# Layer 1 of a four-layer decoder: head-strided attention as steps behind each batch's self-attention

## The chip, the cores and the metric

The kernel runs on one core of a Trainium2 chip. The metric is the device time of one execution in microseconds (us); the reported time is the median of several runs. Engines are named as in the profile: PE multiplies matrices (PEld is its weight load), DVE, ACT and POOL are the vector, scalar and general-purpose engines, SP issues loads and stores. "L568" is line 568 of the kernel before.

## The reference, cut to what matters

The whole is a decoder of four layers. Each layer applies three residual steps to `x` (4 batches of 256 rows by 128 columns): a self-attention, a cross-attention to a context of 4 x 512 rows, and a feed-forward part. The change touches layer 1, whose first two steps are these (16 heads of 8 columns):

```python
def _L1_attn_ref(x, Wqkv, Wout):
    q, k, v = ...                                   # 16 heads, no biases
    scores = jnp.einsum('bhtd,bhsd->bhts', q, k) * SCALE
    scores = jnp.clip(scores, -10.0, 10.0)
    mask = jnp.triu(jnp.full((t, t), NEG), k=1)
    attn = jax.nn.softmax(scores + mask, axis=-1)
    out = jnp.einsum('bhts,bhsd->bhtd', attn, v)
    return out.reshape(b, t, d) @ Wout.T

def _L1_xattn_ref(hidden_states, key_value_states, Wq, bq, Wk, bk, Wv, bv, Wo, bo, stride):
    Q, K, V = ...                                   # projections with biases, 16 heads
    idx = jnp.arange(H)[:, None] + stride * jnp.arange(m)[None, :]
    Kg, Vg = ...                                    # head h sees only keys h, h + 16, h + 32, ...
    attn = jax.nn.softmax(jnp.einsum('bhqd,bhkd->bhqk', Q, Kg) * scaling, axis=-1)
    out = jnp.einsum('bhqk,bhkd->bhqd', attn, Vg)
    return out.reshape(B, Tq, E) @ Wo.T + bo

x = x + _L1_attn_ref(_layernorm(x), L1_attn_Wqkv, L1_attn_Wout)
x = x + _L1_xattn_ref(_layernorm(x), ctx_1024, ..., 16)
x = x + _L1_ffn_ref(_layernorm(x), ...)             # 8 experts, the best 2 per row
```

In the head-strided attention every head sees 32 of the 512 keys, so 16 heads by 32 keys give 512 scores per query row.

## The kernel before

All data stay on the chip as float32: `x` is one tile of 128 partitions by 8 row tiles, two per batch, and the transposed context `cT` has been made in layer 0. The layers run one after the other. Layer 1 is called by `layer_1` (L1753, the self-attention), then `strided_attention` (L1216), then `ffn1` (L1148, the experts). Each stage opens its own pools of on-chip tiles and of PSUM buffers (the banks that PE writes), and closes them at its end.

The self-attention is written by `woven` (L432). A unit is one batch. Its `prelude` (L648) normalises the batch (`normalised_T`, L311), transposes it and projects queries (L449) and keys (L460). Queries are kept four times, each copy multiplied on POOL by a mask that leaves one head of every four (L458). `columns_of` (L547) makes scores with the keys on the partitions: four PE tiles at a time (L568), DVE clips them against -10 and 10 or the causal mask (L578), ACT takes the exponential (L583). `weighted` (L598) multiplies by the values (L604), ACT copies the sums (L610), and `divided_by_sums`, `transposed_result` and `added` (L612 to L646) divide, transpose, project with the output weights (L639) and add to `x` (L643). One batch in layer 1 has two pairs of key-tile groups: in each pair, first a group whose four tiles have 512 score columns, then one with 256, because the causal mask removes the rest.

The order of the steps is a list of (time, function) pairs. `back` (L720) gives the scores of a unit their beats within 0 to 1, and the later steps times after them, each later by a `step`, one beat of the unit; items at or after 1 are carried into the next unit (L750 to L759). All score tiles and other short PSUM tiles of this stage use one set of seven buffers named `s1`. A scheduler then orders the instructions of every engine by their readiness as it estimates it, except those marked with `keep_in_program_order`. [...]

`strided_attention` builds keys and values for all batches first. Keys are spread into blocks, so that one product gives the scores of four heads (`kbd`, L1223 to L1239), and so are values (`vbd`, L1241 to L1265). The query weights are padded: each head has 32 columns, of which 8 are filled, so the query projection is four products per batch (`project`, L336) and DVE adds the bias and scales four times (`padded_queries`, L328). Then, for each of a batch's two row tiles: four score products (L1273), the maximum (L1279) and its subtraction (L1281) on DVE, the exponential on ACT (L1285), four transposes (L379), four products with the values (L1289), division, transposition, output product and addition (`divided`, L360, and `finish`, L352).

The weights of layers 1 to 3 are loaded by `loads` (L1789), eight transfers issued one after the other on ACT within the prelude of the third batch of layer 1: `w1x`, `e1h`, `e1d`, `w2a`, `w2x`, `w3a`, `w3x`, `w3f`. `ternary_weights` (L1647) is called at the end of `linear_attention` (layer 2). It begins with two sums of absolute values of `w3f` on DVE (L1653), which the scheduler may place anywhere after that load was issued.

## Time and profile before

| | us |
|---|---|
| median of 3 runs | 1777.98 (1774.26 to 1781.84) |
| the profiled execution | 1781.78 |
| its span in the profile | 1780.0 |

| engine | busy us | share of the span |
|---|---|---|
| PE | 1459.3 | 82% |
| PEld | 783.2 | 44% |
| DVE | 870.1 | 49% |
| ACT | 694.4 | 39% |
| POOL | 337.2 | 19% |

The clock granted to PE was 0.86 of full speed over the span. The stages around the change, as the timeline shows them: the last write of layer 0's experts is issued at about 384 us, the first score columns of layer 1 begin at 415.5 us, the self-attention's results are added to `x` at 462.6, 476.4, 492.6 and 498.4 us, the last strided result at 582.6 us, and the first product of the experts begins at 608.1 us.

A line of the timeline gives start, duration, engine, line, operation, output and inputs, shapes and count, and in square brackets how long the engine had been idle before it and what released it. A line of the groups gives line, engine, operation, names, shapes and count, then the busy time in us and the mean duration in ns, then the idle time just before it with its releasers. PE counts a float32 product as two instructions and a transpose as one. The chain of waits lists start, duration and what the last-ending chain of work did there.

### The profile page before, as it was taken

Reading aid. Unit: us, or ns where it says so; the run is one execution under the profiler, and the core shown is the slowest. Engines: PE = TensorE matmul, PEld = TensorE weight load, DVE = VectorE, ACT = ScalarE, POOL = GpSimd, SP = SyncE. Lnnn points to the kernel's source line nnn. Section 1 sums busy time; section 2 is a strip of 40 time slices with the busy share of each in tenths; the row PEclk is TensorE's granted clock in tenths of the full one; section 3 lists DMA queues with packets and bytes.
Section 4 is the critical chain, followed back from the end, with each engine's and each line's share of the span. In section 5 each row is a group of like instructions: output and inputs, shape, how many; then the busy total and the mean of one; then the engine's idle time right before and its main releaser. Section 6 shows DMA issues by size and latency. Waiting matters only on the chain.

```text
span 1780.0 us, 27163 instructions
## 1 busy us (share of the span) xinstructions
PE 1459.3 (82%) x10180; PEld 783.2 (44%) x10180; DVE 870.1 (49%) x2888; ACT 694.4 (39%) x1380; POOL 337.2 (19%) x494
## 2 busy tenths in 40 slices
PE   5999987964877694557899999999959569999973
PEld 3443333642356363443444554555536334433322
DVE  5676634332644444547534434444233356765426
ACT  1546562322521131002657565666612114444440
POOL 4231102534130223422000000000023242311000
PEclk9999997986766697558999999999979759999985
DMA  7000002325000111000000000000031200000000
GB/s 283 2 1 1 2 1 111 71 47 221 19 1 0 29 38 27 12 1 7 1 0 1 1 1 1 1 1 1 1 117 43 56 13 2 1 1 2 1 2 11
DMA packets 27183, 50.40 MB, mean 28 GB/s; under 512 B 4275, under 2 KB 20955, under 8 KB 25259
## 3 DMA queue, kind: packets, MB, share of 16 engines
q1 hardware_dynamic: 21902, 30.15, 4.8%
q0 software_dynamic: 4000, 8.20, 2.4%
q10 hardware_dynamic: 1152, 10.33, 1.4%
q8 instruction: 82, 1.34, 0.3%
q14 instruction: 47, 0.39, 0.1%
HBM read 40.96 MB, written 7.70 MB: 27 GB/s over the span
## 4 chain that ended last, share of the span: by engine, by line
PE 70%; DVE 12%; ACT 5%; POOL 5%; DMA 3%; issue 3%; ACTq 0%; POOLq 0%; DVEq 0%
PE s L568 6%; PE g L1014 6%; PE o L604 6%; PE s L503 5%; PE o L1575 5%; PE s L1555 5%; PE f L1504 4%; PE y L1035 3%; PE s L555 3%; PE f L1462 2%; PE f L1490 2%; PE s L562 2%; PE t L1024 2%; POOL back L1077 2%; PE s L1548 1%
## 5 line engine op out<-in xcount | busy, mean ns | idle before, releaser
L568 PE MATMUL s<-qm,kc 32*128 32x512 f32 (+1 forms) x896 | 219.2, 619 | 12.8 <-DVE cl L578 12.8
L503 PE MATMUL s<-kc,qm 32*128 32x256 f32 (+1 forms) x1024 | 219.0, 568 | 11.5 <-POOL qm L458 6.5
L585 ACT ACTIVATE pr<-s 128x512 f32<-128x512 f32 x256 | 138.0, 596 | 196.6 <-PE s L568 192.9
L294 POOL TENSOR_SCALAR ve<-mv 128x2 f32<-128x2 f32 (+1 forms) x64 | 14.9, 233 | 832.4 <-DVE mv L292 768.0
L510 DVE TENSOR_REDUCE mx<-s 128x1 f32<-128x512 f32 (+1 forms) x192 | 122.6, 684 | 73.1 <-PE s L568 60.2
L1515 ACT ACTIVATE ss<-ss,ntop 128x768 f32<-128x768 f32 x128 | 118.6, 927 | 100.5 <-DVE ntop L1513 100.2
L604 PE MATMUL o<-pr,v 128*32 128x256 f32 (+1 forms) x1792 | 145.0, 394 | 10.7 <-ACT os L610 5.4
L1509 DVE CUSTOM_DVE_ANT_0 ss<-f,n 128x512 f32<-128x512 f32 x128 | 83.7, 688 | 80.2 <-PE f L1504 80.2
L503 PEld LDWEIGHTS s<-kc,qm 32*128 32x128 f32 x1024 | 89.7, 210 | 66.3 <-issue 18.5
L1575 PE MATMUL o<-pr,v 128*64 128x256 f32 x768 | 112.5, 400 | 0.0
L514 DVE CUSTOM_DVE_ANT_0 junk<-s,nmif 128x512 bf16<-128x512 f32 x128 | 82.9, 688 | 54.8 <-PE s L503 54.5
L1555 PE MATMUL s<-qT,kT 64*128 64x256 f32 x768 | 106.4, 391 | 0.0
L994 POOL DMA_INDIRECT xb<-sent,token x85 | 80.7, 949 | 135.8 <-PE t L1001 59.1
L458 POOL TENSOR_SCALAR qm<-q,consts 128x256 f32<-128x256 f32 x80 | 72.5, 923 | 172.7 <-ACT q L455 119.5
L587 ACT ACTIVATE pr<-s,n 128x512 f32<-128x512 f32 x128 | 80.0, 689 | 55.3 <-PE s L568 36.3
L604 PEld LDWEIGHTS o<-pr,v 128*32 128x32 f32 x1792 | 40.4, 110 | 118.3 <-issue 83.1
L1562 ACT ACTIVATE pr<-s,n 128x512 f32<-128x512 f32 x128 | 80.5, 678 | 27.7 <-PE s L1555 27.6
L562 PE MATMUL s<-mT,selg 12*128 12x256 bf16 x768 | 82.2, 279 | 2.2 <-ACT mT L283 0.7
L568 PEld LDWEIGHTS s<-qm,kc 32*128 32x128 f32 x896 | 70.9, 201 | 22.9 <-DVE cl L578 14.8
L1504 PE MATMUL f<-kT,qT 64*128 64x512 f32 x256 | 78.5, 627 | 2.4 <-ACT kT L283 1.2
L1026 DVE COPY hT<-t 128x512 f32<-128x512 f32 (+1 forms) x85 | 48.0, 565 | 64.4 <-PE t L1024 64.4
L1575 PEld LDWEIGHTS o<-pr,v 128*64 128x64 f32 x768 | 49.1, 138 | 62.7 <-issue 32.7
(381 smaller groups left out, 2642.5 us busy)
## 6 DMA issues: line engine op xcount, KB each, us to landing
e0h<-in_e0h SPq DMA_DIRECT2D x8, 1024.0 KB, 17.3
done<-ys SPq DMA_DIRECT2D x19, 256.0 KB, 2.8
e0d<-in_e0d SPq DMA_DIRECT2D x1, 4096.0 KB
e1h<-in_e1h ACTq DMA_DIRECT2D x1, 4096.0 KB
w2x<-in_w2x ACTq DMA_DIRECT2D x1, 2050.0 KB
e1d<-in_e1d ACTq DMA_DIRECT2D x1, 2048.0 KB, 17.7
e2h<-in_e2h SPq DMA_DIRECT2D x1, 2048.0 KB, 8.4
e2d<-in_e2d SPq DMA_DIRECT2D x1, 2048.0 KB, 13.8
```

The costliest lines, as they stand in the source:

```text
L503: T.matmul(sc[:, i, :], lhsT=u.qm[r, g + i, qt * P : (qt + 1) * P], rhs=u.kc[r, :], start=u.row_mask is None, stop=True,)
L510: V.tensor_reduce(u.mx[:, qt, j, g : g + per], sc, AX.X, ALU.max)
L562: T.matmul(sc[:, i, :], lhsT=selg[r, gp + i, :], rhs=u.mT[r, :], start=u.cols_mask is None and i == 0, stop=False,)
L568: T.matmul(sc, lhsT=u.kc[r, kt * P : (kt + 1) * P], rhs=u.qm[r, gp : gp + 2, first:], start=u.clip, stop=True,)
L585: A.activation(dst, sc, AF.Exp)
L604: T.matmul(u.po[gp][32 * j : 32 * j + 32, i, first:], lhsT=u.v[:, kt, 4 * j + gp + i, :], rhs=u.pr[gp, kt, j][:, i, first:], start=kt + i ...
L1014: T.matmul(p, lhsT=xbT[b], rhs=wh[:, bass.ds(at_h + 512 * i, 512)], start=biases is None, stop=True,)
L1504: T.matmul(sc[h], lhsT=qT[u, c][hrow[h], qt * P : (qt + 1) * P], rhs=kT[u, c][hrow[h], :SK], start=True, stop=True,)
L1509: V.tensor_tensor_reduce(ss[qt][h][:, :SK], sc[h], neg1[:, b * SK : (b + 1) * SK], 1.0, -3e38, ALU.add, ALU.max, accum_out=mx[:, qt, h, 1:2],)
L1515: A.activation(ss[qt][h], ss[qt][h], AF.Exp, bias=ntop[:, qt, h, c : c + 1], accum_out=total[:, qt, h, c : c + 1],)
L1555: T.matmul(sc[h][:, i, :], lhsT=kT[u, c][hrow[h], kt * P : (kt + 1) * P], rhs=qT[u, c][hrow[h], :], start=False, stop=i == 1,)
L1575: T.matmul(po[u, g][hrow[h], i, :], lhsT=v[u][:, kt, n * hd : (n + 1) * hd], rhs=pr[u, g, kt, h][:, i, :], start=kt + i == 0, stop=kt + i ...
```

## The change

- The head-strided attention is no stage of its own any more. `strided_keys` gives steps that prepare keys and values; they are put beside the scores of the first two batches. `strided_steps` gives nine steps per batch, which are put behind the batch's self-attention (`u.after`), spread over 0.9 of a unit. They use the `s1` buffers and the tiles of the self-attention's stage.
- Queries are no longer padded: one product per batch, ACT adds the bias and scales (`q`), POOL multiplies by the four masks (`qs`). Heads are assigned to blocks in another order, so value and output weights are permuted on the host.
- Both row tiles of a batch share one division, one transposition step and one addition.
- In `back`, the distance between the later steps is half a beat where a unit has four beats or fewer. Carried items may be carried again.
- The two sums of `ternary_weights` are kept in program order.
- `w1x` (now 257 KB instead of 644 KB) is loaded by SP at the end of layer 0's experts, `w2x` by ACT within the second batch of the linear attention, into the memory that the experts of layer 1 leave. The six other loads are put beside the scores of the third batch.

```diff
+            u.beside, u.after = [], []
...
+            out += spread(units[n].beside, 0.0, 1.0)
...
             step = 1.0 / most
+
+            lag = step if len(out) > 4 else 0.5 * step
...
-                late += [(at, call(weighted, u, gp, kt, 0)), (at + step, call(weighted, u, gp, kt, 1))]
+                late += [(at, call(weighted, u, gp, kt, 0)), (at + lag, call(weighted, u, gp, kt, 1))]
...
+            late += [(at + lag, call(transposed_result, u)), (at + 2 * lag, call(added, u))]
+            late += spread(u.after, at + 2.1 * lag, at + 2.1 * lag + 0.9)
...
-            own, late, step = back(n)
-            run(own + front(n) + carried + [i for i in late if i[0] < 1.0])
+            own, late = back(n)
+            items = own + front(n) + carried + late
+            run([i for i in items if i[0] < 1.0])
...
-            carried = [((at - 1.0) * following, f) for at, f in late if at >= 1.0]
+            carried = [((at - 1.0) * following, f) for at, f in items if at >= 1.0]
...
+        def source():
+            u["xnT"] = normalised_T(b, pool, tag="s1", on=G)
+            add_bias(2 * b, 5)
+            add_bias(2 * b + 1, 5)
+
+        def queries():
+            q = pool.tile([P, S], F32, tag="q", name="q")
+            A.activation(
+                q, product(w[:, 0:128], u["xnT"], "s1"), AF.Identity, bias=q_bias, scale=SCALE8
+            )
+            u["q"] = pool.tile([P, 4, S], F32, tag="qs", name="qs", bufs=1)
+            for g in range(4):
+                G.tensor_scalar(u["q"][:, g, :], q, gmask[:, g : g + 1], None, ALU.mult)
+
+        def scores(qt):
+            sc = ps("s1")
+            for g in range(4):
+                T.matmul(
+                    sc[:, g * P : (g + 1) * P], lhsT=u["q"][:, g, qt * P : (qt + 1) * P],
+                    rhs=kbd[:, g, b].rearrange("p j k -> p (j k)"), start=True, stop=True,
+                )
+            sv = sc.rearrange("p (h k) -> p h k", h=H)
+            nm = small.tile([P, H], F32, tag="nmh", name="nmh")
+            V.tensor_reduce(nm, sv, AX.X, ALU.max, negate=True)
+            p = u["p", qt] = pool.tile([P, 512], F32, tag="p", name="p")
+            V.tensor_tensor(
+                p.rearrange("p (h k) -> p h k", h=H), sv,
+                nm.unsqueeze(2).to_broadcast([P, H, nj]), ALU.add,
+            )
+            A.activation(p, p, AF.Exp)
...
+        return [
+            source, queries, call(scores, 0), call(scores, 1), call(turned, 0), call(turned, 1),
+            weighted, turned_back, added,
+        ]
...
         for m in range(2):
-            V.tensor_reduce(
+            tc.keep_in_program_order(V.tensor_reduce(
                 sums[:, m : m + 1], w3f[:, m * 512 : (m + 1) * 512], AX.X, ALU.add,
                 apply_absolute_value=True,
-            )
+            ))
...
-            units[2].prelude.append(loads)
+            kbd, vbd, prepare = strided_keys(pool, w)
+            units[0].beside = prepare[:3]
+            units[1].beside = prepare[3:]
+            units[2].beside = [loads]
+            q_bias = scaled(pool, w[:, 512:513])
+            for u in units:
+                u.after = strided_steps(pool, w, q_bias, kbd, vbd, u.b)
             woven(pool, units, S)
...
+        w1x = load("w1x", pool=late, on=nc.sync)
+
+        def loads():
+            for k in ("e1h", "e1d", "w2a", "w3a", "w3x", "w3f"):
+                held[k] = load(k, pool=experts if k[0] == "e" else late, on=A)
+
+        layer_1(w1x, loads)
+        w2a, w3a, w3x, w3f = (held[k] for k in ("w2a", "w3a", "w3x", "w3f"))
+        ffn1(held["e1h"], held["e1d"])
+    with tc.tile_pool(name="w2x", bufs=1) as experts:
+        other(linear_attention)
+        latent_attention(held["w2x"])
```

The steps `turned`, `weighted`, `turned_back` and `added` do for both row tiles what L379, L1289, `divided` and `finish` did for one, and `strided_keys` does what L1223 to L1265 did, in steps of two block groups of keys and of one batch of values.

## The prediction

> **What bounds the kernel now.** I read the page first (busy shares, slices, chain), then the windows of the stretch that the change touches, then the timeline inside it. Everything else keeps its instructions in the same order: layer 0, its experts, layer 3 and the last feed-forward are untouched in the compiled order. On the page PE is busy 82% of the span, but the clock row drops in the slices that hold this stretch, so it is read by itself:

> ```profile
> 415.50:448.90 33.40, 19.07 (x115) 7.94 (x114) 10.62 (x26) 8.60 (x20) 6.15 (x8) 0.70 0.75 310
> 448.90:498.40 49.50, 41.77 (x348) 20.12 (x348) 32.00 (x93) 27.47 (x59) 6.43 (x11) 0.82 0.01 1
> 498.40:582.90 84.50, 64.76 (x288) 51.93 (x288) 37.76 (x97) 13.50 (x34) 14.72 (x33) 0.63 0.00 0
> ```

> The columns are stretch, length, busy time of PE, PE weight loads, DVE, ACT, POOL, then the granted clock, DMA share, GB/s. First row: self-attention of layer 1 from its first score columns on, with PE busy 19.1 of 33.4 us. Second: the rest of it, PE busy 84% at clock 0.82; PE and its hand-offs set the pace. Third: the head-strided attention, PE busy 77% at only 0.63.

> The first row is poor because of one wait. The chain of waits and the timeline:

> ```profile
> 424.49 23.21 DMA w3f<-in_w3f
> ```

> ```profile
> 447.72 1.28 DVE L1653 TENSOR_REDUCE sums<-w3f 128x1 f32<-128x512 f32 x2 [17.84 <-DMA w3f<-in_w3f]
> 449.65 2.41 PE L568 MATMUL s<-qm,kc 32*128 32x256 f32 x6 [12.83 <-DVE cl L578]
> ```

> A reduction for the ternary weights of the *last* layer stands early in DVE's queue and waits for the last of eight weight loads. DVE is idle for 17.84 us, then PE for 12.83 us because DVE frees no score buffers. The groups of the strided stage:

> ```profile
> L340 PE MATMUL sc<-xnT,w1x 128*128 128x256 f32 x32 | 14.5, 610 | 0.0
> L1289 PE MATMUL ms<-vbd,pT 128*128 128x36 f32 x64 | 13.7, 378 | 4.1 <-DVE pT L281 2.3 <-ACT pT L283 1.8
> L1273 PE MATMUL sc<-kbd,qT 128*128 128x128 f32 x64 | 13.3, 370 | 2.0 <-DVE qT L333 2.0
> L379 PE MATMUL pt<-consts,p 128*128 128x128 f32 x32 | 7.3, 373 | 5.3 <-ACT p L1285 5.3
> L1248 PE MATMUL ms<-w1x,kg 128*128 128x32 f32 x32 | 7.1, 353 | 1.4 <-POOL kg L1247 1.3
> L333 DVE TENSOR_SCALAR qT<-sc,w1x 128x256 f32<-128x256 f32 x16 | 6.7, 477 | 14.0 <-PE sc L340 14.0
> ```

> [...]

> **The change part by part.**

> *Ternary sums pinned.* In the compiled order they now stand in the linear attention, after its last transposed result. Without the wait DVE's next tile would have been ready at about 432.2 (scores begun at 431.54, a first pair takes 0.65); it resumed at 448.9. That is 16.7 us, less some 1.7 because four score tiles then lay ready: −15. The reductions cost 1.3 at their new place, partly beside eight projections: take +1 (0 to +1.4).

> *Strided stage leaves as a stage.* −84 us (498.4 to the last x<-x,ms at 582.6).

> *Its work comes back inside the self-attention.* PE: per batch before, groups divided by four: projections 3.6, scores 3.3, weighted 3.4, transposes of p 1.8, output 1.4, small transposes 1.5: 15. The unpadded query projection is one product instead of four (0.9), so 12 at clock 0.63, about 7 at full clock. DVE loses four qT (1.7 per batch), POOL gains four masks. The rows L458 and L298 of the trace price POOL: 0.92 for a 128x256 mask, 0.78 for a normalised tile.

> The compiled order of PE decides how much of this is hidden. Per batch it reads: self output (as L639), weighted sums, transposes of xn, four score tiles, query product, transposes of the self result, strided scores, four score tiles, and so on to the strided output. I walk from the end of one batch's self output to the next, with the durations of before:
> - x add 0.42, statistics 0.8, POOL ve and rs 1.1, two xn 1.6, hand-offs 0.4: xn is ready at 4.3. In PE's queue only 0.9 to 1.6 us of weighted sums stand ahead of its transposes, so PE waits about 3 us.
> - xnT, query product, ACT q behind two exponentials: q at 7.2. POOL's four masks take 3.6: the last strided score can start at 10.9. Ahead of it PE has only transposes (0.7 to 1.1) and one weighted sum: another wait of about 3 us.
> - From there: scores and the next four tiles 3.3, transposes of p with one wait on the second exponential 2.0, four tiles 0.7, weighted 2.6, and the rest to the next self output 8.4.

> Sum: 28 us per batch with PE at full clock, 34 with every PE piece at the slow durations seen (score tiles 3.0 for 2.2, weighted 3.8 for 2.2, transposes 1.1 for 0.66). [...] I take 31. Before, one batch took 14.2 (49.5 us hold seven pairs of score groups, 7.1 each) plus 17.5 in the strided stage.

> Now the stretch:
> - Head to the first score columns: 415.5 before. POOL's memset of kbd (1.84) and two key copies now stand behind the four gathers, ahead of the first normalisation: +1 (0 to +2).
> - To the first batch's self output: 3.5 score groups at 7.1 = 25, key and value preparation on PE 9 (2.0 + 7.1), waits of the doubled kg buffer 2, one score buffer held for the values 1: 37, so 453.5.
> - Two periods of 31: 515.5.
> - Third strided batch mixed with the last self result, nothing else left to cover it: from the walk, 24: 539.5.
> - Fourth strided batch alone, every hand-off exposed: normalise 4.3, xnT, product and q 1.9, masks 3.6, scores to second p 2.5, then exponential, transposes, copy twice (ACT has them in that order) 4.6, weighted 1.9, divide, transpose, output, add 3.3, hand-offs 2.4: 24.5, so 564.

> 564 against 582.6 is −18.6.

> *Loads.* The strided weights come on SP ahead of the last write of the expert results: at worst its 257 KB go first, 0 to +1.5; ACT's copies for the last two writes end at 380.4 and 384.3, which leaves room, so 0. The other loads move to the middle of the third batch, some 60 us before the experts need e1h; their six issues cost ACT 3 us where it has slack: 0. The 2 MB of w2x now load beside the linear attention's gathers (2.5 us each, on its chain): 0 (−1 to +3).

> *Same lag rule elsewhere.* The halved lag applies only where a unit has four beats, which is layer 1; the carried items of layers 0 and 3 keep their order. 0.

> Sum: −18.6 + 1.0 = about −17.5. On the profiled execution, 1781.8, this gives 1764; on the median of the runs, 1778.0, it gives 1760.5. I forecast **1762**.

> **Rivals.**
> - *The strided work truly fills gaps.* If POOL and DVE deliver earlier than I walked, PE is the bound: 14.2 + 7 = 21 to 22 per batch at a higher clock, tails 22 each: 450 + 44 + 44 = 538, −45: **1735**. For: PE is idle 23% in the strided stage[...]. Against: the two places in PE's queue with too little ahead.
> - *The interleaving pays back most of the stall.* Period 34, preparation 40, tails 26 and 27: 579, −4 and +1: **1777**. For: 0.63 in the strided stage although no wait there is long.
> - *Slower.* All strided tiles share the seven s1 buffers, four of which one score group needs. Two strided score tiles, a transposed tile and the value tile can hold four, so the next group waits for DVE, in whose queue the strided maxima stand between the clipped tiles. It decides from a period of 40 on (582.6 − 453.5 − 48.5, halved); at 45 the stretch ends at 592: **1789**. For: PE already waits on L578. Against: the value tile is held in the first two batches only.

> **How the numbers follow.** Forecast 0.62, gaps filled 0.14, paid back 0.16, slower 0.08. The forecast's own range takes its ends: 548 with full clock and short tails (−35, 1743), and 572 with a slow clock (−10, 1772). To leave out no more than 2 in 10 I reach up to the paid-back case: 1742 to 1780. What this kernel's measurement can tell from no change is about 0.5%, 9 us: below 1769 is faster. That takes 0.56 of the forecast and all of the first rival: 0.70; same 0.22; slower 0.08.

> **What would show it.** Right: no DVE wait on w3f; a strided chain whose last add comes near 564; about 30 us between self outputs, with PE waiting twice per batch, for xn and for the masked queries; 49 us from the third self output to the end of the stage; granted clock near 0.7. Wrong: a wait of DVE or POOL on a load in this stretch, score tiles waiting for free buffers, periods under 25 us, or a linear attention longer by over 3 us.

## The result, and the profile after

The changed kernel takes 1766.22 us (median of 4 runs, 1763.65 to 1770.69) against 1777.22 us for the kernel before (4 runs, 1774.26 to 1781.84): a ratio of 0.9938, 95% interval 0.9909 to 0.9968. In a second comparison, with more runs, it was 0.9955 (0.994 to 0.997). So it is faster by about 0.5%. The forecast was 1762; the profiled execution was to go from 1781.8 to 1764, and it went to 1770.7 (span 1768.9).

The windows of the changed kernel, cut at the adds that end each batch: to the first self output, to the second, third and fourth, and to the last strided add. Columns as in the prediction:

```profile
415.10:458.40 43.30, 38.60 (x253) 21.16 (x256) 18.67 (x46) 19.52 (x40) 15.06 (x26) 0.63 0.00 1
458.40:488.20 29.80, 22.72 (x168) 13.78 (x172) 15.20 (x38) 11.43 (x25) 6.97 (x10) 0.83 0.31 122
488.20:516.40 28.20, 23.22 (x164) 13.62 (x162) 14.69 (x37) 11.16 (x24) 6.97 (x10) 0.76 0.34 141
516.40:543.70 27.30, 17.97 (x104) 13.62 (x102) 7.85 (x24) 5.28 (x12) 6.97 (x10) 0.74 0.00 1
543.70:568.50 24.80, 14.44 (x50) 10.74 (x50) 6.68 (x24) 3.17 (x6) 9.70 (x16) 0.50 0.00 0
```

The stretch from the first score columns to the last strided add is 153.4 us, where it was 415.5 to 582.6, 167.1 us. The wait for w3f is gone, so one would expect the first interval to be short: it was 47.1 us with the 17.8 us wait in it (first self output at 462.6), and is still 43.3 without. The next three intervals cost 27 to 30 us each, and the lone last one has its clock at 0.50.

PE in the timeline around the second period shows what the queue looks like (a float32 product counts as two instructions: the 32 strided score products of the stage are x64, so x16 are eight):

```profile
487.41 0.71 PE L578 MATMUL s<-w1a,oT 128*128 128x128 f32 x4 [2.18 <-ACT oT L272]
488.06 1.66 PE L543 MATMUL o<-pr,v 128*32 128x256 f32 x10
491.39 0.47 PE L297 MATMUL s<-consts,xn 128*128 128x128 f32 x1 [1.68 <-POOL xn L287]
...
496.75 5.07 PE L1241 MATMUL s<-kbd,qs 128*128 128x128 f32 x16
```

PE waits for the self result's copy, then for the normalised rows. The eight strided score products show no wait ahead of them but take 5.07 us; POOL writes the four masked queries that they read from 495.64 on, 3.62 us long. Part of the wait lies between the products. The granted clock is 0.50 there; in later runs eight such products took 3.78 us in one piece at 0.50 (550.69, masks on DVE), and six took 1.60 us at 1.00 (456.00, value products moved). Over the whole stretch, the groups (busy time, mean ns, then idle time ahead of them):

```profile
L507 PE MATMUL s<-qm,kc 32*128 32x256 f32 (+1 forms) x128 | 23.7, 737 | 0.0
...
L1241 PE MATMUL s<-kbd,qs 128*128 128x128 f32 x64 | 18.9, 450 | 6.0 <-POOL qs L1236 5.1
```

The self-attention's score products (L507) never wait, for a buffer or anything else.

What was gained is partly given back at the end of the linear attention. DVE there, in the changed kernel:

```profile
788.14 0.38 DVE L1398 COPY aT<-pt 128x128 f32<-128x128 f32 x1 [0.57 <-PE pt L1397]
788.37 1.25 DVE L1662 TENSOR_REDUCE sums<-w3f 128x1 f32<-128x512 f32 x2
...
791.62 0.48 DVE L1675 TENSOR_SCALAR wt<-w3f,wr 128x512 f32<-128x512 f32 x1
```

and in the kernel before:

```profile
799.25 0.48 DVE L1666 TENSOR_SCALAR wt<-w3f,wr 128x512 f32<-128x512 f32 x1
...
800.50 0.38 DVE L1388 COPY aT<-pt 128x128 f32<-128x128 f32 x1 [0.23 <-PE pt L1387]
```

Before, with the sums known long ago, the first ternary weights were made in DVE's waits ahead of the last transposed copy (aT). With the sums pinned behind that copy, all of it comes behind, between the output products. From that copy to the next stage's mask load it was 5.2 us (800.50 to 805.67) and is 7.6 (788.14 to 795.77). The copy itself now follows the one before it after 5.5 us instead of 5.9, so 2.0 us are lost in all.

Put together, from the profiles: stretch −13.7, its start −0.4, experts and their gathers up to the first transposed copy of the linear attention +2.2, the linear attention up to the mask load +2.0, everything after that −1.2: −11.1, as between the two spans (1780.0 and 1768.9). The last term is noise: the part from the mask load on, whose instructions are the same, took between 967.5 and 975.0 us in the twelve profiles. For this reason the experiments are read by stages as well as by totals.

### The profile page after: what moved, and what is told of

It is laid out like the page before. It is cut to its first block, busy times and chain, and to the rows that moved or that the text cites. A ratio compares the mean times of both kernels' runs of the same rounds, so it can differ in the third digit from the quotient of the medians.

```text
span 1768.9 us, 27091 instructions
## 1 busy us (share of the span) xinstructions
PE 1448.3 (82%) x10156; PEld 774.9 (44%) x10156; DVE 855.8 (48%) x2847; ACT 695.3 (39%) x1374; POOL 360.0 (20%) x518
## 4 chain that ended last, share of the span: by engine, by line
PE 48%; DVE 7%; POOL 4%; ACT 4%; issue 3%; DMA 1%; POOLq 0%; ACTq 0%; DVEq 0%
PE o L1584 5%; PE s L1564 5%; PE g L958 4%; PE f L1513 4%; PE s L507 3%; PE o L543 3%; PE s L494 3%; PE s L442 3%; PE f L1471 2%; PE y L979 2%; PE f L1499 2%; PE s L1557 1%; PE f L1458 1%; POOL back L1021 1%; ACT ss L1524 1%
## 5 line engine op out<-in xcount | busy, mean ns | idle before, releaser
L507 PE MATMUL s<-qm,kc 32*128 32x512 f32 (+1 forms) x896 | 213.7, 622 | 0.0
L283 POOL TENSOR_SCALAR ve<-mv 128x2 f32<-128x2 f32 (+1 forms) x64 | 15.0, 234 | 816.8 <-DVE mv L281 752.2
L526 ACT ACTIVATE pr<-s,n 128x512 f32<-128x512 f32 x128 | 80.0, 689 | 52.1 <-PE s L507 33.1
L1571 ACT ACTIVATE pr<-s,n 128x512 f32<-128x512 f32 x128 | 80.5, 678 | 28.5 <-PE s L1564 28.4
L1584 PEld LDWEIGHTS o<-pr,v 128*64 128x64 f32 x768 | 48.9, 137 | 62.4 <-issue 32.1
L1506 DVE CUSTOM_DVE_ANT_0 ss<-f,nought 128x256 f32<-128x256 f32 x128 | 46.7, 421 | 58.3 <-PE f L1499 58.2
```

The source lines that it names most:

```text
L507: T.matmul(sc, lhsT=u.kc[r, kt * P : (kt + 1) * P], rhs=u.qm[r, gp : gp + 2, first:], start=u.clip, stop=True,)
L1584: T.matmul(po[u, g][hrow[h], i, :], lhsT=v[u][:, kt, n * hd : (n + 1) * hd], rhs=pr[u, g, kt, h][:, i, :], start=kt + i == 0, stop=kt + i ...
```

## The experiments

The first four ask where the gain comes from. The letters in their expectations: A says that the pin alone brings it and that the interleaving brings nothing of its own; its rivals give the interleaving a gain, and C says that this gain is held up by the masks on POOL.

**The pin alone.** The kernel before, with only this:

```
-            V.tensor_reduce(
+            tc.keep_in_program_order(V.tensor_reduce(
                 sums[:, m : m + 1], w3f[:, m * 512 : (m + 1) * 512], AX.X, ALU.add,
                 apply_absolute_value=True,
-            )
+            ))
```

> The kernel before, with nothing but the two ternary sums kept in program order. Theory A (the pinned sums brought the gain, the interleaving about nothing): the 17.8 us wait of DVE goes, the last strided add comes 16 us earlier (near 567), the sums cost 2 to 3 us at the end of the linear attention; 1761 to 1765, level with the changed kernel. Rival B (the interleaving brought it, the wait was partly covered): 1770 to 1775, clearly slower than the changed kernel's 1766.

1765.63 us (6 runs) against 1779.38: ratio 0.9906 (0.9879 to 0.9933). Its windows: to the first and second self output, then the strided stage up to its first row tile, its preparation included, and its other seven row tiles:

```profile
420.30:451.90 31.60, 27.72 (x197) 12.36 (x200) 19.10 (x49) 17.55 (x40) 9.77 (x12) 0.77 0.79 327
451.90:465.80 13.90, 12.49 (x115) 5.67 (x108) 10.06 (x28) 8.59 (x19) 0.94 (x2) 0.88 0.01 5
...
487.20:513.90 26.70, 20.93 (x109) 16.98 (x109) 11.04 (x26) 6.75 (x20) 11.04 (x25) 0.56 0.00 1
513.90:571.57 57.67, 43.85 (x179) 35.01 (x179) 26.46 (x70) 6.75 (x15) 3.68 (x8) 0.65 0.00 0
```

The stretch ends at 571.57 after 151.3 us, 15.8 less than before. The pin alone does all that the whole change does, as A expected. From the last transposed copy to the mask load it too takes 7.7 us.

**The change without the pin.** The same edit taken out of the changed kernel.

> The changed kernel with the sums left to the scheduler. They stand in DVE's queue within the third batch and must wait for w3f, issued last of six loads near 482 and landing some 18 us later. Theory A: DVE waits 10 to 16 us there and the kernel takes 1776 to 1782, the time of before. Rival B: the wait is covered by strided work, 1766 to 1770.

1776.2 us (22 runs), ratio 0.9981 (0.9971 to 0.9991). DVE in its timeline:

```profile
485.58 2.48 DVE L517 SCALAR_TENSOR_TENSOR cl<-s,upto 128x512 f32<-128x512 f32 x4 [0.63 <-PE s L507]
501.88 1.28 DVE L1662 TENSOR_REDUCE sums<-w3f 128x1 f32<-128x512 f32 x2 [13.82 <-DMA w3f<-in_w3f]
```

The wait is back, one batch later, because the load of w3f is now issued at 482.9 us instead of 424.5. The stretch is 167.4 us, as before the change (167.1), although this wait is 4 us shorter than that one (13.8 for 17.8). So what the change does beyond the pin is small. Without the pin it is worth 0.2% (0.1 to 0.3%, some 3 us). Beside the pin no gain is seen: the pin alone has a ratio of 0.9906, the whole change 0.9938 and 0.9955.

**The strided steps as a stage of their own**, with everything else of the change kept:

```
-                u.after = strided_steps(pool, w, q_bias, kbd, vbd, u.b)
+                u.late_steps = strided_steps(pool, w, q_bias, kbd, vbd, u.b)
             woven(pool, units, S)
+            for u in units:
+                for f in u.late_steps:
+                    f()
```

> The changed kernel with the strided steps of all batches after the self-attention, in the same pool, instead of behind each batch. Theory A (interleaving brings little, since PE waits in order for POOL twice per batch): within 5 us of the changed kernel either way. Rival B (interleaving hides much of the strided work): slower by 12 us or more, 1778 and above.

1776.36 us (21 runs), ratio 0.9983 (0.9971 to 0.9995). By the ratios it is 5 to 8 us slower than the changed kernel, between the 5 us within which A puts it and the 12 us of its rival.

```profile
413.43:455.56 42.13, 37.77 (x253) 21.08 (x256) 18.52 (x46) 19.05 (x40) 15.14 (x26) 0.67 0.00 1
455.56:491.81 36.25, 25.82 (x280) 12.83 (x279) 23.94 (x73) 19.70 (x43) 7.65 (x14) 0.95 0.52 210
491.81:572.56 80.75, 55.31 (x200) 42.46 (x198) 19.69 (x48) 12.69 (x24) 23.02 (x32) 0.50 0.00 0
```

Its stretch is 159.1 us. So interleaving by itself does gain, 6 us (153.4) to 9 us (150.0, the second profile below). The rewriting loses as much, 8 us against the pin alone (151.3): a strided batch takes 80.75/4 = 20.2 us here, with one query product and four masks on POOL, where the padded one of the kernel before took 17.7 (adds at 518.35, 536.04, 553.99, 571.57 in the run with the pin alone). PE is idle for 6.4 us of such a batch, where it was 4.3. It has fewer products, and yet it is busy for 13.8 us, where it was 13.4: the granted clock is 0.50 here and was 0.60 to 0.69 there. How much of the 2.5 us is the clock's was not separated.

**Masks on DVE.** From PSUM in one operation, without ACT's copy (`acc` is the query product in PSUM, `gmask8` the masks times the scale):

```
+            acc = product(w[:, 0:128], u["xnT"], "s1")
...
-                G.tensor_scalar(u["q"][:, g, :], q, gmask[:, g : g + 1], None, ALU.mult)
+                V.tensor_scalar(
+                    u["q"][:, g, :], acc, w[:, 512:513], gmask8[:, g : g + 1], ALU.add, ALU.mult
+                )
```

> The changed kernel, but DVE makes the four masked queries of the strided part straight from PSUM (bias, then mask times scale: 4 x 0.48 us), in place of an ACT copy and four POOL products (0.46 + 3.6 us). Theory C (PE's queue stands still for the masked queries): PE's wait before the strided scores falls by 2 to 2.5 us in each of four batches, 1756 to 1760. Rival D (PE's own work or DVE bounds the stretch): 1765 to 1768, and DVE's 8 us more show.

1765.86 us (6 runs), ratio 0.9908 (0.9882 to 0.9933). The median is one that D expects; as a ratio it lies 5 to 8 us below the changed kernel (0.9938 and 0.9955), near what C expects. So the total does not decide. The stages show more: the stretch is 147.0 us, the last two intervals 24.1 and 21.2 where the changed kernel has 27.3 and 24.8. The last batch can be compared directly, since the granted clock is 0.50 around these products in both. First the changed kernel, then this one:

```profile
552.56 5.20 PE L1241 MATMUL s<-kbd,qs 128*128 128x128 f32 x16 [2.52 <-POOL qs L1236]
...
550.69 3.78 PE L1240 MATMUL s<-kbd,qs 128*128 128x128 f32 x16 [0.64 <-DVE qs L1233]
```

The wait ahead of the eight products and the products themselves together take 4.4 us instead of 7.7. Some 3 us per batch were POOL's, as C says; the first period did not gain (32.5 us at a clock of 0.79, where the changed kernel has 29.8 at 0.83; the last section has two like batches at different clocks).

The next three, with the changed kernel beside them, ask about the first interval and how much of the rest can be had.

**The changed kernel again.**

> The changed kernel once more, unaltered, beside the three variants below: a median ratio to the kernel before of 0.993 to 0.995 (first measured 0.9938), and in the profile 153.4 us from the first score columns of layer 1 to the last strided add, within 1 us, wherever that stretch begins. If the stretch differs by more than 1 us between two runs of one kernel, then differences of 2 us between kernels (the pin alone took 151.3) say nothing.

1766.69 us (22 runs), ratio 0.9955 (0.994 to 0.997). The stretch was 150.0 us, not within 1 us of 153.4: two batches ran at a higher clock (28.5 us at 0.88 and 26.2 at 0.93, where they had 29.8 at 0.83 and 28.2 at 0.76), and the other three intervals agree within 0.2. By the expectation's own bound the pin alone (151.3) and the whole change can't be told apart.

**Preparation in the head.** Keys and values for the strided attention made ahead of the self-attention, the memset and the key copies on DVE:

```
-                G.memset(kbd, 0.0)
+                V.memset(kbd, 0.0)
...
-                G.tensor_copy(kg, keys[:, b, :, g : 16 : 4].rearrange("p k j -> p j k"))
+                V.tensor_copy(kg, keys[:, b, :, g : 16 : 4].rearrange("p k j -> p j k"))
...
-            units[0].beside = prepare[:3]
-            units[1].beside = prepare[3:]
+            for f in prepare:
+                f()
```

> The changed kernel with the whole key and value preparation of the strided attention made ahead of the self-attention, while PE waits for the gathers, its memset and sixteen key copies on DVE instead of POOL. If the preparation is what makes the first self output late (43.3 us after the first score columns, against 31.6 with the pin alone), then this interval falls to 31.5 to 34 and the stretch from 153.4 to 142 to 144, the whole by 9 to 11 us. Rival: the interval was set by the clock (granted 0.63 there), and PE without the preparation goes no faster: 38 or more, the whole within 5 us. Third possibility: DVE's copies delay the adds of the gathered rows and the head grows by what the stretch loses: last store of the expert results to first score columns above 32 us.

1755.94 us (6 runs), ratio 0.9894 (0.9865 to 0.9922): 11 us below the changed kernel of the same comparison (1766.69), as expected.

```profile
420.16:450.25 30.09, 24.43 (x189) 11.39 (x192) 17.88 (x44) 16.63 (x36) 9.79 (x12) 0.78 0.00 1
```

The first interval falls by 13.1 us to 30.1, and the stretch to 137.7. So the preparation made this interval long, and not the clock by itself; the clock rose with it, from 0.63 to 0.78. The third possibility came true too: from the last store of the expert results (383.60) to the first score columns it is 36.6 us instead of 31.8. DVE's adds of the gathered rows stand between key copies that wait for PE, and POOL's normalisation waits for them:

```profile
395.55 0.28 DVE L1026 TENSOR_TENSOR x<-x,back 128x128 f32<-128x128 f32 x1
395.94 0.27 DVE L1194 COPY kg<-cT 128x128 f32<-128x128 f32 x1
```
```profile
399.10 0.23 POOL L283 TENSOR_SCALAR ve<-mv 128x2 f32<-128x2 f32 x1 [6.06 <-DVE mv L281]
```

**All of it, with the sums moved.** That head, masks and normalised rows on DVE, and the two sums made in the last batch of the linear attention (the cut shows the sums):

```
                 for i in range(2):
+                    if b == B - 1 and i == 1:
+                        held["sums"] = ternary_sums()
```

> The preparation in the head as in the run before, the masked queries and the normalised rows on DVE, and the two absolute sums made inside the last batch of the linear attention, in a wait of DVE of 3 us for PE, instead of behind its last transposed copy. Expected: the waits for xn (2.7 and 1.7 us per batch) shrink by 1 each and the score products no longer take 5.1 us: periods of 25 to 27, 22 and 20; stretch 134 to 138; from the last transposed copy to the mask load of the next stage 5.2 instead of 7.6 us. The whole 20 us under the changed kernel, near 1746. Rival: DVE, now with everything that POOL did, becomes the bound: periods stay at 27 to 29, stretch 141 to 144, whole 10 us under it.

1752.93 us (6 runs), ratio 0.9866 (0.983 to 0.9901).

```profile
771.83 1.25 DVE L1661 TENSOR_REDUCE sums<-w3f 128x1 f32<-128x512 f32 x2
...
777.52 0.38 DVE L1399 COPY aT<-pt 128x128 f32<-128x128 f32 x1 [0.23 <-PE pt L1398]
...
782.71 0.35 SPq L332 DMA_DIRECT2D mrow<-in_mbf  x1
```

From the last transposed copy to the mask load it is 5.2 us again, with that copy 5.9 us after the one before it, both as before the change: the pin's price was its place. The last two intervals are 23.2 and 20.9, 0.4 to 0.9 us less than with the masks alone. But the two full periods are 33.2 and 28.3 at clocks of 0.69 and 0.88, and the stretch is 135.5, only 2.2 us less than in the run before it. 1746 was not reached.

**The self-attention's masks on DVE as well.** In layer 1 only:

```
+            if u.clip:
+                u.qm = pool.tile([P, 4, S], F32, tag="qm", name="qm", bufs=3)
+                for g in range(4):
+                    V.tensor_scalar(u.qm[:, g, :], acc, u.gmask8[:, g : g + 1], None, ALU.mult)
+                return
```

> The same, and the masked queries of the self-attention of this layer made by DVE from the product, without ACT's copy and POOL's four masks. In the head POOL was the queue that decided (25.5 of 32.1 us busy, two times four masks of 0.92 ahead of gathers): 7 us shorter there, first score columns some 25 us after the last store of the expert results instead of 31.9; stretch as in the run before or 1 to 2 us longer, since DVE has four products of 0.47 more per batch. The whole near 1740. Rival: the gathers' own latency sets the head, and it shortens by 2 us or less.

1742.54 us (5 runs), ratio 0.9824 (0.9792 to 0.9856): the fastest of all, about 24 us below the changed kernel of the same comparison (1766.69). The head is 31.9 us (380.37 to 412.26), 4.6 less than in the run before; in POOL's queue the gathers of the second pair of batches no longer stand behind masks:

```profile
396.84 1.58 POOL L287 TENSOR_SCALAR xn<-x,mv,rs 128x128 f32<-128x128 f32 x2
398.59 1.09 POOL L1026 DMA_INDIRECT back<-done,index  x1 [0.17 <-issue]
```

The 25 us hoped for were counted from the changed kernel's 31.9; the preparation had made the head 36.5 in the run before, and of the 7 us expected 4.6 came. The stretch is 130.9 us. That is 4.6 less than in the run before, but 2.9 of it lie in one period that ran at a clock of 0.96 instead of 0.88.

**The value products behind the second batch's queries**, to free the head of them:

```
+            first += spread(units[0].early, 0.85, 1.0)
...
-            for f in prepare:
+            for f in prepare[:3]:
                 f()
+            units[0].early = prepare[3:]
```

> As the run before (masks, normalised rows and self-attention masks on DVE, sums in the linear attention), but the value products of the strided attention stand behind the second batch's queries, where PE and DVE wait for gathers, instead of ahead of the first gathered rows. There eight pairs of key copies between DVE and PE held the adds of the gathered rows: normalisation on POOL started 5.9 us late. If that is so, the head (last store of the expert results to first score columns) falls from 31.9 to 27 to 28 us and the whole by 4 us. Rival: the copies then delay the second batch's normalisation by as much and the head stays at 31 to 32. Stretch from first score columns to last strided add as before, 131, with 3 us either way for the clock.

1750.43 us (6 runs) against 1780.16, ratio 0.9848 (0.9819 to 0.9877). The rival held, the head is 30.9 us: the first normalisation on POOL starts 4.6 us sooner after the last store (10.7 us for 15.3), but the second then waits for its statistics, which stand between key copies:

```profile
408.63 0.23 POOL L283 TENSOR_SCALAR ve<-mv 128x2 f32<-128x2 f32 x1 [5.98 <-DVE mv L281]
```

And the last copies spilled into the first score tiles, which then ran one product at a time; in the run before, four products (x8) took 2.09 us at the same granted clock of 0.50:

```profile
411.93 2.07 PE L512 MATMUL s<-qm,kc 32*128 32x512 f32 x2
413.93 1.06 PE L1202 MATMUL s<-w1x,kg 128*128 128x32 f32 x4
414.92 2.07 PE L512 MATMUL s<-qm,kc 32*128 32x512 f32 x2
```

The first interval is 37.5 us instead of 28.6, the stretch 139.6. Moved this way, the work only changed its place.

**The same with the strided steps as a stage of their own.**

> The run beside it with the strided steps of all four batches behind the self-attention instead of in its chain. It asks what the interleaving is worth once the masks are on DVE. From the parts measured so far: self-attention alone 29 + 14 + 14 + 7.5 us, four strided batches at 20.1 less 3.5 for the masks, less 0.5 for the normalised rows, 64: stretch 128 to 130, no longer than interleaved (131). With masks on POOL the own stage was 6 to 9 us longer. If the interleaving truly covers waits then this one is again 6 us or more longer; if PE's queue only exchanges one wait for another, the two are within 3 us.

1759.26 us (6 runs), ratio 0.9885 (0.9856 to 0.9914). The four strided batches take 17.3 us each (493.41 to 562.43; 20.2 with the masks on POOL, 17.7 padded), but the stretch is 147.5, not 128 to 130: the expectation took 29 for a first interval that was 36.7, as in the run beside it, and 14 for periods that were 17.4 and 16.4 (14.7 and 14.1 in the earlier run with its own stage; why they grew was not tried). Against 139.6 the interleaving is worth 8 us with the masks on DVE too, and the medians differ by 8.8: it does cover waits.

## Why the prediction was right, and where not

The direction was right, and so was the main cause, the wait for w3f. Of the size two thirds came: −17.5 was forecast for the profiled execution and −11.1 came, and the medians differ by 11. (The 1762 lies between the two values that the sum gives, 1760.5 from the median and 1764 from the profiled execution; of the range's ends the lower is counted from the one, the upper from the other.) Its steps:

- *Pinned sums, −15.* Right: the pin alone takes 15.8 us off the stretch.
- *Sums at their new place, +1 (0 to +1.4).* Too small: +2.5 behind the last transposed copy and +2.0 in all, outside its bound. The step counted the two reductions and missed what depends on them: the scalings and roundings that DVE had done in waits ahead of the last transposed copy went behind it. Moving the sums ahead of that copy brought the 5.2 us back.
- *Strided stage into the chain, −84 and back, −3.6 beyond the pin* (−18.6 with it). Measured against the pin alone it is +2.1 in one profile and −1.3 in the other: nothing that two profiles of one kernel, 3.4 us apart, could tell. The forecast came out because the pin carried nearly all of it. That interleaving gains (6 to 9 us) and the rewriting loses as much (20.2 for 17.7 us per batch) was not in it as two terms.
- *Head, +1.* +0.7 (31.2 to 31.9).
- *To the first self output, 37: 25 + 9 + 2 + 1.* It took 43.3. The term that failed is the 25: without preparation the interval is 31.6 us (pin alone) and 30.1 (preparation in the head). The steady 7.1 per score group was used for the filling of the pipeline, at a clock of 0.77. The profile of before had the answer: 47.1 us to its first self output, less the 15 of the wait, is 32. Preparation, 12 in the sum, measured 11.7 and 13.1.
- *Two periods of 31.* 29.8 and 28.2, then 28.5 and 26.2: on average 28.2, the lower end of the walk's 28 to 34, and less than taken; where between those ends a period would lie was an estimate of the author's. The wait for xn is there (1.7 to 2.7 us), the one for the masks too, inside 5.07 us of products; the one for the self result's copy (2.2) was not walked.
- *Third strided batch 24.* 27.3 in both profiles: it was taken from the walk at full clock and ran at 0.74. *Fourth alone 24.5*: 24.8.
- *The stretch, 147.5 from its first score columns.* 153.4. The first interval was 6.3 us longer than summed, the two periods 4.0 shorter, the two tails 3.6 longer. That the misses have both signs is luck.
- *Loads 0, lag rule elsewhere 0.* Nothing against them is seen: no wait for w1x, w2x or the six loads in this stretch, and the linear attention, beside which w2x now loads, takes 80.3 us from its first to its last transposed copy, where it took 80.7. Experts and gathers together took 2.2 us longer; the cause stays open.
- *Its signs.* The last strided add came at 568.5 for 564, the end 52.1 us after the third self output for 49, and the granted clock of the stretch was 0.69 for the estimated 0.7. None of the signs against it came.
- *Rivals.* "Gaps filled" did not come with masks on POOL; with them on DVE and the preparation out of the stream, the stretch of 130.9 us goes that way (the rival had 122.5). Of score tiles waiting for buffers, as the slower rival wanted, there is none (L507, 0.0).

## What to carry to other kernels

When a change bundles an edit that removes a stall with a large rearrangement, price each against a version that has only the other: here one wrapped call brought the gain, and the large rearrangement was worth 0.3% at most without it and nothing measurable beside it. A pinned instruction takes along all that depends on it, so pin it where its followers still find idle time (from the last transposed copy to the mask load 7.6 us with the sums behind that copy, 5.2 with them ahead of it). And before moving work from PE to another engine to save PE time, ask who waits for the last piece: in a stage of its own a strided batch took 17.7 us with three more products and no masks, 20.2 with four masks of 0.92 us on POOL, and 17.3 with masks and normalised rows on DVE (granted clocks 0.66, 0.50 and 0.55).

## What the runs showed of the hardware

In the run with the value products moved, two neighbouring batches have the same instructions in nearly the same order, and the one with the lower granted clock of PE took 6.8 us longer:

```profile
449.38:475.40 26.02, 20.38 (x168) 11.76 (x167) 16.77 (x43) 10.94 (x24) 1.84 (x4) 0.96 0.35 141
475.40:508.23 32.83, 28.23 (x166) 16.42 (x169) 16.68 (x42) 10.74 (x23) 1.83 (x4) 0.69 0.29 121
```

In the second, the eight weighted products of the strided part take 3.63 us, at a clock of 0.50, instead of 2.09 at 1.00. PE is the busier in the second batch (86% at 0.69, against 78% at 0.96), so a high busy share was no sign of a high clock here: it was high because the products were slow. The same time, cut where the clock changes:

```profile
448.29:451.70 3.41, 2.84 (x20) 1.27 (x20) 1.14 (x6) 0.54 (x2) 0.95 (x2) 0.50 0.00 0
451.70:475.59 23.89, 18.82 (x156) 11.45 (x158) 15.83 (x38) 10.94 (x24) 0.90 (x2) 1.00 0.38 154
475.59:485.83 10.24, 9.09 (x47) 4.94 (x40) 5.80 (x19) 1.50 (x4) 1.83 (x4) 0.50 0.92 382
485.83:492.66 6.83, 5.23 (x35) 2.90 (x33) 4.69 (x8) 2.80 (x6) 0.00 (x0) 1.00 0.01 4
492.66:502.90 10.24, 10.24 (x60) 6.84 (x59) 2.76 (x10) 3.69 (x9) 0.00 (x0) 0.50 0.01 2
```

Both batches run at 0.50 near their start, behind a wait of PE for the self result's copy: the first, with a wait of 1.68 us, for 3.41 us, the second, with 2.61, for 10.24.

```profile
448.18 1.09 PE L583 MATMUL s<-w1a,oT 128*128 128x128 f32 x4 [1.68 <-DVE oT L270]
474.65 0.71 PE L583 MATMUL s<-w1a,oT 128*128 128x128 f32 x4 [2.61 <-ACT oT L272]
```

The second runs at 0.50 once more, from 492.66 on, through the slow weighted products. Ahead of them PE waits 1.25 and 0.35 us for the exponentials, exactly as in the first batch, where the clock stayed at 1.00. The first two rows are the first batch, with one of the two waits in each; the third row is the second batch, with both in it:

```profile
458.53:461.94 3.41, 2.17 (x17) 0.98 (x16) 3.18 (x6) 1.29 (x3) 0.00 (x0) 1.00 0.00 0
461.94:465.35 3.41, 2.83 (x24) 2.03 (x24) 2.69 (x6) 3.41 (x8) 0.00 (x0) 1.00 0.00 0
489.25:492.66 3.41, 1.81 (x17) 0.99 (x14) 3.41 (x7) 2.25 (x6) 0.00 (x0) 1.00 0.00 0
```

What set the clock was not shown, nor whether it is why one kernel's stretch took 153.4 us once and 150.0 us once.
